# A mixture-of-experts tail with half-size tiles: tile plan, table in pieces, and results scattered by halves

## Chip, cores and metric

The kernel runs on one core of a Trainium2 chip. The metric is device time in microseconds (us) from the first to the last instruction, as the median of three runs. All arithmetic is float32, so every product on TensorE appears in the trace as two matmul records with two weight loads.

## The reference

The input is an image batch `x` of shape (2, 256, 56, 56). Layer 0 is a group norm, a convolution that makes queries, keys and values, a windowed attention and a projection. Layer 1 turns the image into 6272 tokens of 256 features, runs a linear attention with a feed-forward block, and then a mixture of experts. The change is about that last part:

```python
logits = xt @ Wr + br                         # 6272 tokens, 8 experts
top_p, top_idx = jax.lax.top_k(softmax(logits), 2)
weights = top_p / top_p.sum(axis=-1, keepdims=True)
xe = xn[None] * ln_g[:, None, :] + ln_b[:, None, :]
h = gelu(einsum('end,edh->enh', xe, W1) + b1[:, None, :])   # 256 -> 1024
y = einsum('enh,ehd->end', h, W2) + b2[:, None, :]          # 1024 -> 256
out = (weights[:, :, None] * y_of_the_two_chosen).sum(axis=1)
t = t + out
```

Every token goes to 2 of the 8 experts, so there are 12544 (token, expert) rows. How many fall to each expert depends on the data.

## The kernel before

**Stages.** `front` does layer 0. `layer1` does the rest of the attention in groups of tokens, up to 4 blocks of 128 tokens each, in the order of the list `order`: eleven groups of four blocks, then groups of one, two and two blocks, 14 groups and 49 blocks in all. For each group there are generators: `queries` (q), `message` (m), `feed_forward` (f) and `route` (r); `route` has three steps, and the third of the group before is called p. A string of letters for each step `s` says in which order TensorE gets their parts: `turns` for the steps with new groups, `last` for the steps that drain the pipeline. TensorE's order is the written one (`manual_schedule`); the other engines' queues are ordered by a scheduler.

**Routing.** `route` normalises a group, computes the router (L1663), picks two experts (`top_two`, L1592), counts the rows of each expert in `cnt`, and scatters each token's normalised row twice into a table `xs` in HBM with indirect DMAs on GpSimd (POOL). Each expert has its own region in `xs`.

**Experts.** Class `Experts` works on tiles of `ST` = 256 rows of one expert. Which expert and which rows a tile takes is decided on the chip: `full_tiles` (L1195), called once after the first `NE` = 36 blocks have been counted, makes a table A of `NTA` = 29 tiles that are certainly full by then; `other_tiles` (L1209), called in the fifth tile of the main loop, makes a table B for all further ones from the final counts, and writes one block of filler rows behind each expert's rows (8 DMAs). Both use `table` (L1149), a chain of small VectorE (DVE) instructions. A tile goes through these steps:

- `fetch` (L1235): SyncE (SP) reads the tile's expert and row from the table into registers, then issues four DMAs in this order: the rows `xr` (260 KB), the weights `w1e` and `w2e` (1 MB each) and the bias `b2e`. The weights have two buffers, so `w1e` of a tile can only be loaded once the first product of the tile two before it is done, and `w2e` once its second product is done. DVE makes the weight of each row (`eq`) and its token number (`idi`, two buffers).
- `turn` (L1274): 4 transposes on TensorE (`px`), then two DVE instructions that apply the expert's norm (`xe`).
- First product: 8 output pieces of 2 matmuls 128x128 by 128x256 (L1303), each followed by a Gelu on ScalarE (ACT, L1307).
- Second product: for each half of 128 rows 8 matmuls 128x128 by 128x256 (L1316).
- Result: one DVE add of the bias over both halves (L1323), then for each half a multiply by the row's weight on POOL (L1330) and an indirect DMA that adds the half onto `y2` in HBM (L158).

`NTL` = 56 tiles are enough for any counts. Three of them (0 to 2) are mixed with the end of the attention by the letter `e` in `last`; tiles 3 to 52 form the main loop; tiles 53 to 55 stand under a condition (`tc.If`, L1828) that is taken if the counts ask for them.

**Output.** From tile `NTE` = 43 on, `between` (L1810) reads a finished group of `y2` back (`read`, L1782) after the first product of each tile, and `write` (L1792) transposes the group read one tile before, copies it out of PSUM on ACT and stores it to `out` from the ACT queue. After the last tile the five remaining groups are read and written one after the other; the read buffers `yr` and the copies `o_sb` have two and three buffers.

Of the kernel before, what the change touches and what calls it, by code (L numbers as in the profile page):

```python
# [18 lines left out]
P = 128  # L19
# [28 lines left out]
NIF = 3  # L48
# [3 lines left out]
NE = 36  # L52
NTA = -(-(NE * P * K - E * (ST - 1)) // ST)
NTE = (NE * P * K + E * (ST - 1)) // ST
NTB = NTL - NTA
NFI = 3
# [3 lines left out]
def shape_constants():  # L60
# [24 lines left out]
    def key_masks(n, nk):  # L85
# [20 lines left out]
        "c_tile": np.tile(np.arange(NTA, dtype=np.float32), (P, 1)),  # L106
# [10 lines left out]
def hybrid_kernel(ctx: ExitStack, tc: tile.TileContext, a: dict, out: bass.AP):  # L117
# [981 lines left out]
    class Experts:  # L1099

        def __init__(self, ctx, tk):
# [12 lines left out]
            self.tnum = self.load("tnum", a["c_tile"], [P, NTA])  # L1116
            self.enum = self.load("enum", a["c_e"], [P, E])

# [11 lines left out]
        def counts(self, pc, ones, name):  # L1130

            nc.tensor.matmul(pc, ones, self.tk.cnt, start=True, stop=True)
            ce = self.wp.tile([P, E], F32, name=name)
            nc.vector.tensor_copy(ce, pc)
            return ce

        def steps_below(self, wp, ce, k0, op, name):

            ns = N // ST + 1 - k0
            gt = wp.tile([P, E, N // ST + 1], F32, name="gt")[:, :, :ns]  # L1140
            nc.vector.tensor_tensor(
                gt, ce.unsqueeze(2).to_broadcast([P, E, ns]),
                self.steps[:, k0:].unsqueeze(1).to_broadcast([P, E, ns]), op,
            )
            n = self.wp.tile([P, E], F32, name=name)
            nc.vector.tensor_reduce(n, gt, AX.X, ALU.add)
            return n

        def table(self, wp, name, tiles, nt, start):  # L1149
# [6 lines left out]
            nc.vector.tensor_reduce(incl, cum, AX.X, ALU.add)  # L1156

# [7 lines left out]
            nc.vector.tensor_tensor(more, base[:, 1:], base[:, :ns], ALU.subtract)  # L1165
            ge = wp.tile([P, tiles, ns], F32, name=f"ge{name}")
# [8 lines left out]
            nc.vector.tensor_scalar(et, et, float(E - 1), None, ALU.min)  # L1175
            etm = wp.tile([P, tiles], F32, name=f"etm{name}")
# [3 lines left out]
            nc.vector.tensor_tensor(ge, ge, more.unsqueeze(1).to_broadcast([P, tiles, ns]), ALU.mult)  # L1180
            rt = wp.tile([P, tiles], F32, name=f"rt{name}")
# [5 lines left out]
            nc.vector.tensor_copy(tab[:, 1, :], rt)  # L1187
            oh = wp.tile([P, tiles, E], F32, name=f"oh{name}")
# [6 lines left out]
        def full_tiles(self, pc, ones):  # L1195

            ce = self.counts(pc, ones, "ce1")
            nt = self.steps_below(self.wp, ce, 1, ALU.is_ge, "full")
            self.some = self.steps_below(self.wp, ce, 0, ALU.is_gt, "some")
            self.tab_a = self.table(self.wp, "A", NTA, nt, self.ebase)  # L1200

# [7 lines left out]
        def other_tiles(self, wp, pc):  # L1209
            ones = wp.tile([P, P], F32, name="ones4")  # L1210
            nc.vector.memset(ones, 1.0)
            ce = self.counts(pc, ones, "ce2")
# [4 lines left out]
            nc.vector.tensor_copy(endi, endf)  # L1217
            for e in range(E):
                r = self.value(endi[0:1, e : e + 1], E * RG - ST)
                ins = nc.sync.dma_start(xs[bass.ds(r, ST), :], a["c_fill"][e])  # L1220
                apart(ins.ins, [f"fill{self.tk.run}"], [f"xs{self.tk.run}", f"xfull{self.tk.run}"])
            n = self.steps_below(wp, ce, 0, ALU.is_gt, "all")
            nt = wp.tile([P, 2, E], F32, name="nt")
            nc.vector.tensor_tensor(nt[:, 0, :], self.some, self.taken, ALU.subtract)
            nc.vector.tensor_tensor(nt[:, 1, :], n, self.some, ALU.subtract)
            start = wp.tile([P, 2, E], F32, name="start")
            for k, t in enumerate((self.taken, self.some)):
                nc.vector.scalar_tensor_tensor(start[:, k, :], t, float(ST), self.ebase, ALU.mult, ALU.add)
            self.tab_b = self.table(
                wp, "B", NTB, nt.rearrange("p k e -> p (k e)"), start.rearrange("p k e -> p (k e)")  # L1230
            )
            self.last = wp.tile([P, 1], mybir.dt.int32, name="last")
            nc.vector.tensor_copy(self.last, self.tab_b.incl[:, 2 * E - 1 :])

        def fetch(self, t, pools):  # L1235

            run = self.tk.run
            full = t < NTA
            tab, k = (self.tab_a, t) if full else (self.tab_b, t - NTA)
            x = SimpleNamespace(t=t)  # L1240
            xr = x.xr = pools.xr()
            e = self.value(tab.tab[0:1, 0, k : k + 1], E - 1)
            r = self.value(tab.tab[0:1, 1, k : k + 1], E * RG + (NDUM - 1) * ST)
            ins = nc.sync.dma_start(xr, xs[bass.ds(r, ST), :].rearrange("(p j) c -> p j c", j=2))
# [16 lines left out]
            nc.vector.tensor_scalar(x.eq, xr[:, :, C + 3], tab.etm[:, k : k + 1], None, ALU.is_equal)  # L1261
            x.idi = self.small.tile([P, 2], mybir.dt.int32, name="idi")
            nc.vector.tensor_copy(x.idi, xr[:, :, C])  # L1263
            nc.vector.tensor_tensor(x.eq, x.eq, xr[:, :, C + 2], ALU.mult)
            nc.vector.tensor_tensor(x.eq, x.eq, xr[:, :, C + 1], ALU.add)
# [8 lines left out]
        def turn(self, x, pools):  # L1274

            px = pools.px()
            for ct in range(2):
                for j in range(2):
                    nc.tensor.transpose(px[:, ct, j, :], x.xr[:, j, ct * P : (ct + 1) * P], ident)
            x.xe = pools.xe()  # L1280
            for ct in range(2):
                nc.vector.tensor_scalar(
                    x.xe[:, ct, :], px[:, ct, :, :].rearrange("p j t -> p (j t)"),
                    x.sv[:, ct : ct + 1], x.sv[:, 2 + ct : 3 + ct], ALU.mult, ALU.add,
                )

        def run(self, ts, pools, between=lambda t: None):
# [3 lines left out]
            nxt = self.fetch(ts[0], pools)  # L1291
# [3 lines left out]
            for t in ts:  # L1295
                x = nxt
                if t < ts[-1]:
                    nxt = self.fetch(t + 1, pools)
                hT = self.w.tile([P, NJ, ST], F32, name="hT")
                for j in range(NJ):  # L1300
                    p1 = pools.ph()
# [8 lines left out]
                between(t)  # L1310
                if t < ts[-1]:
                    self.turn(nxt, pools)
                py = pools.py()
                for h in range(2):
                    for j in range(NJ):
# [4 lines left out]
                        if j % 4 == 3 and (h, j) != (1, NJ - 1):  # L1320
                            yield
                yt = pools.yt()
                nc.vector.tensor_tensor(yt, py, x.b2.unsqueeze(1).to_broadcast([P, 2, C]), ALU.add)  # L1323
                mine, others = [f"y{run}.{t}"], [f"y{run}.{t}"]
                if t < NTA:
                    mine, others = mine + [f"yfull{run}"], others + [f"ylate{run}"]
                if t >= NTE:
                    mine, others = mine + [f"yend{run}"], others + [f"yread{run}"]
                for h in range(2):
                    nc.gpsimd.tensor_scalar(  # L1330
                        yt[:, h, :], yt[:, h, :], x.eq[:, h : h + 1], 1.0, ALU.mult, ALU.mult
                    )
                    scatter(y2, x.idi[:, h : h + 1], yt[:, h, :], mine, others, compute_op=ALU.add)
                yield


    def layer1(ctx, tk, behind=(None, None)):
# [16 lines left out]
        early = next(i for i in range(len(order)) if sum(n for _, n in order[:i]) == NE)  # L1354
        with lin as ph:
# [195 lines left out]
            def feed_forward(n0, n, m2T):  # L1551
# [13 lines left out]
                for k0 in range(0, n, 2):  # L1565
# [22 lines left out]
                    if (n0, n) in order[early:]:  # L1588
# [41 lines left out]
            def route(n0, n):  # L1630
# [57 lines left out]
                late = [f"xlate{run}"] if (n0, n) in order[early:] else []  # L1688
# [25 lines left out]
            last = "mefefpefmeferefer", "fefefpeferefeer", "eeeeprer", "eeeep"  # L1714
# [3 lines left out]
            with tc.manual_schedule(engines={mybir.EngineType.PE}):  # L1718
                on = {}
                for s in range(ng + 4):  # L1720
# [12 lines left out]
                    for part in turns[min(s, 2)] if s < ng else last[s - ng]:  # L1733
                        if part == "e":
                            next(tiles, None)
                        else:
                            next(on.get(part, iter(())), None)
                        if part == "p" and s == early + 3:
# [3 lines left out]
                            ex.full_tiles(ps_a.tile([P, E], F32, name="pc", tag="a"), ones)  # L1742
# [9 lines left out]
                            tiles = ex.run(range(NFI), pools)  # L1752
                            next(tiles)
# [10 lines left out]
        with ExitStack() as ph:  # L1764
            xp = ph.enter_context(tc.tile_pool(name="p4x", bufs=3, reuse_waits="tile"))
            yp = ph.enter_context(tc.tile_pool(name="p4yr", bufs=2, reuse_waits="tile"))
# [25 lines left out]
            def write(n0, n, yr, copy):  # L1792
                for ct in range(2):
# [5 lines left out]
                    o_sb = xp.tile([P, 512], F32, name="o_sb")  # L1799
                    copy(o_sb[:, : n * P], pt[:, : n * P])  # L1800
                    for b in range(B):
                        c0, c1 = max(n0 * P, b * T), min((n0 + n) * P, (b + 1) * T)
                        if c0 < c1:
                            nc.scalar.dma_start(
                                ov[b, ct, :, c0 - b * T : c1 - b * T], o_sb[:, c0 - n0 * P : c1 - n0 * P]
                            )

            held = []

            def between(t):  # L1810
                if t == NFI + 2:
                    ex.other_tiles(tp, ps_t.tile([P, E], F32, name="pc", tag="pt"))
                if t == NFI + 4 and run == 0:
                    check_sums(tp, ps_t)

                if t > NTE and held:
                    write(*held.pop(0), nc.scalar.copy)
                if NTE <= t < NTE + early:
                    held.append(read(*order[t - NTE], True))

            with tc.manual_schedule(engines={mybir.EngineType.PE}):
                for _ in ex.run(range(NFI, NTL - NIF), pools, between):
                    pass
            behind = nc.values_load(
# [64 lines left out]
```

## Time and profile before

| | |
|---|---|
| runs | 2144.49, 2147.65 and 2149.08 us |
| profiled execution | span 2144.9 us (2146.76 us by the clock of the runs) |
| TensorE (PE) busy | 1979.2 us, 92% of the span |
| DVE, ACT, POOL busy | 1007.1, 635.1, 692.1 us |
| expert tiles executed | 53 (1696 records each on L1303 and L1316) |
| first product, second product | 380.4 and 376.3 us busy |
| bytes moved by DMA | 265.93 MB, 124 GB/s over the span |

"Busy" is time with an instruction in progress. The slices of the page show busy tenths of an engine in 40 equal parts of 53.6 us; PEclk is the clock that TensorE was granted. In the timeline, a bracket at the end of a line says how long the engine stood idle before it and what released it. A row with PE gives the matmuls, PEld the weight loads, SPq and ACTq the issue of DMAs.

### The profile page before, as it was taken

The numbers are of one execution on the slowest core, as the hardware profiler recorded it, in microseconds if no ns is written. First come the engines' busy times: TensorE is split into PE (matmuls) and PEld (weight loads), VectorE is DVE, ScalarE is ACT, GpSimd is POOL, SyncE is SP. The second block draws the span as 40 slices with busy tenths as digits, with TensorE's granted clock in tenths as the row PEclk, the third lists the DMA queues.
The fourth block names the chain that finished last, engine by engine and source line by source line (L and its number), as shares of the span: only waits on it lengthen the run. The fifth ranks groups of instructions, "written<-read, shape, count | busy, mean of one in ns | idle before, by whom it ended". The sixth has DMA issues, their size and how long they took to land.

```text
span 2144.9 us, 27983 instructions
## 1 busy us (share of the span) xinstructions
PE 1979.2 (92%) x10190; PEld 1391.2 (65%) x10190; DVE 1007.1 (47%) x2538; ACT 635.1 (30%) x1256; POOL 692.1 (32%) x810
## 2 busy tenths in 40 slices
PE   6799989999988887999999979899999999999995
PEld 3454444554544555666656657688888888888884
DVE  6777877875986556455454454321111111111110
ACT  1233323233333222333233322322222222222231
POOL 4721012111013425345344444433323333233231
PEclk9999999999989999999999998999999999999997
DMA  5642422443243113001111131577666766677883
GB/s 130 156 105 74 144 73 65 116 124 87 88 133 80 49 29 109 11 21 40 35 50 48 50 131 48 173 221 212 196 186 199 200 192 188 195 204 207 251 242 98
DMA packets 189461, 265.93 MB, mean 124 GB/s; under 512 B 25335, under 2 KB 148549, under 8 KB 189071
## 3 DMA queue, kind: packets, MB, share of 16 engines
q1 hardware_dynamic: 161694, 221.74, 34.3%
q0 software_dynamic: 21296, 30.41, 7.2%
q10 hardware_dynamic: 6320, 11.86, 1.8%
q8 instruction: 84, 1.38, 0.3%
q14 instruction: 67, 0.54, 0.1%
HBM read 197.01 MB, written 71.21 MB: 125 GB/s over the span
## 4 chain that ended last, share of the span: by engine, by line
PE 30%; issue 25%; DVE 16%; POOL 15%; DMA 6%; ACT 3%; SPq 0%; POOLq 0%; DVEq 0%; ACTq 0%
POOL y L158 7%; PE p L1559 4%; PE py L501 4%; PE pc L513 4%; PE po L566 4%; DMA y<-yt,idi 3%; DVE yc L526 3%; DVE p L557 2%; POOL rs L246 2%; PE s_ps L553 2%; POOL yt L1330 2%; PE kp L277 2%; PE s_ps L350 1%; PE kx L290 1%; PE py L1571 1%
## 5 line engine op out<-in xcount | busy, mean ns | idle before, releaser
L1303 PE MATMUL ph<-xe,w1e 128*128 128x256 f32 x1696 | 380.4, 382 | 13.3 <-ACT hT L1307 9.0
L1316 PE MATMUL py<-w2e,hT 128*128 128x256 f32 x1696 | 376.3, 380 | 0.0
L1303 PEld LDWEIGHTS ph<-xe,w1e 128*128 128x128 f32 x1696 | 323.6, 191 | 58.9 <-ACT hT L1307 9.4
L1307 ACT ACTIVATE hT<-ph,sv 128x256 f32<-128x256 f32 x424 | 201.0, 474 | 540.2 <-PE ph L1303 537.1
L1316 PEld LDWEIGHTS py<-w2e,hT 128*128 128x128 f32 x1696 | 318.6, 190 | 41.3
L526 DVE SCALAR_TENSOR_TENSOR yc<-ypad,w,yc 128x1120 f32<-128x1120 f32 x192 | 267.1, 1394 | 46.8 <-ACT yc L524 43.8
L513 PE MATMUL pc<-ypad,diag 128*128 128x448 f32 x432 | 176.6, 549 | 0.5 <-ACT ypad L507 0.5
L158 POOL DMA_INDIRECT y<-yt,idi x106 | 168.6, 1591 | 25.3 <-issue 16.1
L501 PE MATMUL py<-x_sb,wq 128*128 128x448 f32 (+1 forms) x384 | 157.2, 541 | 14.9 <-ACT yc L517 9.5
L562 ACT ACTIVATE p<-p 98x680 f32<-98x680 f32 (+5 forms) x120 | 111.8, 932 | 179.5 <-DVE p L557 173.7
L557 DVE TENSOR_TENSOR p<-s_ps,tab 98x340 f32<-98x340 f32 (+5 forms) x240 | 137.9, 600 | 56.8 <-PE s_ps L553 55.4
L1263 DVE CAST idi<-xr 128x2 int32<-128x2 f32 x53 | 9.0, 169 | 317.9 <-DMA y<-yt,idi 317.9
L1330 POOL TENSOR_SCALAR yt<-yt,eq 128x256 f32<-128x256 f32 x106 | 49.3, 472 | 310.4 <-DVE yt L1323 305.2
L1323 DVE TENSOR_TENSOR yt<-py,b2e 128x512 f32<-128x512 f32 x53 | 36.6, 692 | 234.9 <-PE py L1316 234.9
L553 PE MATMUL s_ps<-qT,kT 32*98 32x170 f32 (+5 forms) x960 | 130.5, 402 | 16.9 <-DVE p L557 15.6
L553 PEld LDWEIGHTS s_ps<-qT,kT 32*98 32x98 f32 (+1 forms) x960 | 57.4, 170 | 104.3 <-DVE p L557 58.2
L513 PEld LDWEIGHTS pc<-ypad,diag 128*128 128x128 f32 x432 | 78.2, 189 | 71.7 <-issue 67.8
L490 POOL TENSOR_SCALAR diag<-ident,w 128x128 f32<-128x128 f32 x108 | 84.6, 801 | 116.4 <-PE pc L513 109.5
L501 PEld LDWEIGHTS py<-x_sb,wq 128*128 128x128 f32 x384 | 71.0, 198 | 78.7 <-issue 55.5
L158 POOL DMA_INDIRECT xs<-row,si x98 | 96.1, 981 | 64.2 <-DVE si L1687 33.0
L246 POOL TENSOR_TENSOR rs<-rs,mhalf 128x2 f32<-128x2 f32 (+2 forms) x89 | 65.2, 739 | 145.5 <-DVE rs L245 122.6
L1559 PE MATMUL p<-m2T,fw 128*128 128x512 f32 (+2 forms) x224 | 94.3, 544 | 0.0
(326 smaller groups left out, 2594.0 us busy)
## 6 DMA issues: line engine op xcount, KB each, us to landing
w1e<-in_L_ffn_W SPq DMA_DIRECT2D x53, 1024.0 KB
w2e<-in_L_ffn_W SPq DMA_DIRECT2D x53, 1024.0 KB
yd<-yc SPq DMA_DIRECT2D x24, 784.0 KB
xr<-xs SPq DMA_DIRECT2D x53, 260.0 KB
ld<-yd SPq DMA_DIRECT2D x28, 448.0 KB
b2e<-in_L_ffn_b SPq DMA_DIRECT2D x53, 128.0 KB
yr<-y SPq DMA_DIRECT2D x11, 512.0 KB
out<-o_sb ACTq DMA_DIRECT2D x22, 256.0 KB
```

The lines of the kernel that those rows point to most:

```text
L158: ins = nc.gpsimd.indirect_dma_start(out=dst[:, :], out_offset=bass.IndirectOffsetOnAxis(ap=index, axis=0), in_=src, in_offset=None, **kw,)
L246: nc.gpsimd.tensor_tensor(r[:, :n], r[:, :n], mhalf[:, :n], ALU.pow)
L501: nc.tensor.matmul(py[:, :n, :], wq1[:, ct, oc * P : (oc + 1) * P], x_sb[:, ct, (q0 + g0) * WW : (q0 + g0 + n) * WW], start=(ct == 0), sto ...
L513: nc.tensor.matmul(pc, diag[:, tap, :], ypad[:, dy : dy + 8, dx : dx + WW], start=(tap == 0), stop=(tap == 8),)
L526: nc.vector.scalar_tensor_tensor(yc[:, 8:, :], src, w, yc[:, 8:, :], ALU.mult, ALU.add)
L553: nc.tensor.matmul(s_ps[:nk, j, :n].rearrange("p (i j) -> p i j", j=nj), kT[hs], q[hs], start=True, stop=True,)
L557: nc.vector.tensor_tensor(p[:nk, 2 * pr : 2 * pr + 2, :n].rearrange("p h (i j) -> p h i j", j=nj), s_ps[:nk, :, :n].rearrange("p h (i j) - ...
L562: nc.scalar.activation(p[:nk, :, :n], p[:nk, :, :n], AF.Exp)
L1303: nc.tensor.matmul(p1, x.w1[:, ct, j * P : (j + 1) * P], x.xe[:, ct, :], start=(ct == 0), stop=(ct == 1),)
L1307: nc.scalar.activation(hT[:, j, :], p1, AF.Gelu, bias=x.sv[:, 4 + j : 5 + j])
L1316: nc.tensor.matmul(py[:, h, :], hT[:, j, h * P : (h + 1) * P], x.w2[:, j, :], start=(j == 0), stop=(j == NJ - 1),)
L1559: nc.tensor.matmul(p1[:, :w], fw1[:, k, oc * P : (oc + 1) * P], rhs, start=(k == 0), stop=(k == 3))
```

## The change

1. **Tile plan.** 48 full tiles and 5 half tiles (128 rows of one expert) take the place of the 53 full tiles. A half tile has half of the transposes, first products of 128x128 by 128x128, Gelus of 128 columns and one half of the second product; its DMAs of `w1e`, `w2e` and `b2e` are those of a full tile. An expert gets a half tile where its last tile is new after 36 blocks and has 128 rows or less; a third table H lists them. The half tiles stand between the last full ones: 43, h0, 44, h1, 45, h2, 46, h3, 47, h4. Everything beyond 48 full and 5 half tiles (8 full, 3 half) stands under the condition.
2. **First count a group sooner.** Table A is made after 32 blocks (`NE1`), with 25 tiles. The counts after 36 blocks (`NE2`) are kept by a copy (`remember`). The letter strings begin mixing `e` one step earlier.
3. **Tables in pieces.** `table`, `full_tiles` and `other_tiles` are generators, stepped once after each part of the order. `other_tiles` starts in the first tile of the main loop instead of the third, and its eight filler DMAs are issued one by one.
4. **Results by halves.** `turn` makes bias times weight on POOL ahead; after each half of the second product one DVE instruction makes `py * eq + yt`, and that half is scattered at once. `idi` has four buffers.
5. **Output.** `yr` has five buffers, `o_sb` a pool of its own with four. In the loop, the write of the group read before stands ahead of the next read. At the end all five reads are issued first; the two halves of a group are copied by ACT and DVE and stored from the ACT and the SP queue.

```diff
-NE = 36
-NTA = -(-(NE * P * K - E * (ST - 1)) // ST)
-NTE = (NE * P * K + E * (ST - 1)) // ST
+NE1, NE2 = 32, 36
+NTA = -(-(NE1 * P * K - E * (ST - 1)) // ST)
+NTE = (NE2 * P * K + E * (ST - 1)) // ST
+NFS, NHS = 48, 5
...
         def full_tiles(self, pc, ones):
-            ce = self.counts(pc, ones, "ce1")
+            ce = self.counts(self.wp, pc, ones, self.tk.cnt, "ce1")
             nt = self.steps_below(self.wp, ce, 1, ALU.is_ge, "full")
-            self.some = self.steps_below(self.wp, ce, 0, ALU.is_gt, "some")
-            self.tab_a = self.table(self.wp, "A", NTA, nt, self.ebase)
+            yield
+            self.tab_a = yield from self.table(self.wp, "A", NTA, nt, self.ebase)
+            yield
...
         def other_tiles(self, wp, pc):
+            nc.vector.tensor_scalar(fit, n, -float(ST), float(ST - P), ALU.mult, ALU.add)
+            nc.vector.tensor_tensor(fit, fit, ce, ALU.add)
+            nc.vector.tensor_scalar(half, fit, 0.0, None, ALU.is_le)
+            nc.vector.tensor_tensor(half, half, late, ALU.mult)
+            yield
...
+            self.tab_h = yield from self.table(wp, "H", E, half, start[:, 2, :])
...
             for e in range(E):
+                yield
                 r = self.value(endi[0:1, e : e + 1], E * RG - ST)
                 ins = nc.sync.dma_start(xs[bass.ds(r, ST), :], a["c_fill"][e])
...
         def turn(self, x, pools):
...
+            x.yt = pools.yt()
+            for h in range(nh):
+                nc.gpsimd.tensor_scalar(x.yt[:, h, :], x.b2, x.eq[:, h : h + 1], 1.0, ALU.mult, ALU.mult)
...
                 py = pools.py()
-                for h in range(2):
+                for h in range(nh):
                     for j in range(NJ):
                         nc.tensor.matmul(
...
-                        if j % 4 == 3 and (h, j) != (1, NJ - 1):
+                        if j == 3:
                             yield
-                yt = pools.yt()
-                nc.vector.tensor_tensor(yt, py, x.b2.unsqueeze(1).to_broadcast([P, 2, C]), ALU.add)
...
-                for h in range(2):
-                    nc.gpsimd.tensor_scalar(
-                        yt[:, h, :], yt[:, h, :], x.eq[:, h : h + 1], 1.0, ALU.mult, ALU.mult
+                    nc.vector.scalar_tensor_tensor(
+                        x.yt[:, h, :], py[:, h, :], x.eq[:, h : h + 1], x.yt[:, h, :], ALU.mult, ALU.add
                     )
-                    scatter(y2, x.idi[:, h : h + 1], yt[:, h, :], mine, others, compute_op=ALU.add)
-                yield
+                    scatter(y2, x.idi[:, h : h + 1], x.yt[:, h, :], mine, others, compute_op=ALU.add)
+                    yield
...
-            last = "mefefpefmeferefer", "fefefpeferefeer", "eeeeprer", "eeeep"
+            last = "mqefpefemqfreferf", "meffefpemferfer", "fefpfefrefeer", "eeeeperer", "eeeep"
...
+            slots = [(t, 2) for t in range(NFI, NFS)]
+            for k in range(NHS):
+                slots.insert(len(slots) - NHS + k + 1, (k, 1))
+            first = slots.index((NTE, 2))
             held = []
-            def between(t):
-                if t == NFI + 2:
-                    ex.other_tiles(tp, ps_t.tile([P, E], F32, name="pc", tag="pt"))
...
-                if t > NTE and held:
-                    write(*held.pop(0), nc.scalar.copy)
-                if NTE <= t < NTE + early:
-                    held.append(read(*order[t - NTE], True))
+            def between(i):
+                if held:
+                    write(*held.pop(0), (nc.scalar, nc.scalar))
+                if first <= i < first + early2:
+                    held.append(read(*order[i - first], True))
...
-            with tc.If(behind > NTB - NIF):
-                for _ in ex.run(range(NTL - NIF, NTL), pools):
+            with tc.If(more > 0):
+                for _ in ex.run([(t, 2) for t in range(NFS, NTL)] + [(k, 1) for k in range(NHS, E)], pools):
                     pass
-            for h in held:
-                write(*h, evac)
-            for n0, n in order[early:]:
-                write(*read(n0, n, False), evac)
+            last = [read(n0, n, False) for n0, n in order[early2:]]
+            for h in held + last:
+                write(*h, (nc.scalar, nc.sync))
```

## The prediction

> **What bounds the kernel now.** I read the slices of the page first, for where TensorE (PE) isn't full; then busy time by stretches; then the timeline of each stretch that the change touches.
>
> ```profile
> PE   6799989999988887999999979899999999999995
> PEclk9999999999989999999999998999999999999997
> DMA  5642422443243113001111131577666766677883
> ...
> 1250.00:1300.00 50.00, 38.95 (x177) 30.12 (x176) 25.76 (x132) 9.37 (x28) 24.52 (x29) 0.83 0.44 151
> 1350.00:1400.00 50.00, 39.53 (x189) 33.76 (x188) 18.54 (x104) 15.20 (x29) 20.65 (x24) 0.90 0.60 178
> 1600.00:1650.00 50.00, 50.00 (x239) 44.01 (x239) 9.33 (x29) 11.86 (x25) 14.49 (x18) 1.00 0.64 187
> 2000.00:2050.00 50.00, 49.28 (x245) 43.15 (x246) 8.88 (x28) 14.90 (x31) 13.88 (x16) 1.00 0.85 246
> 2110.00:2130.00 20.00, 8.10 (x37) 6.72 (x36) 1.38 (x2) 0.00 (x1) 4.09 (x4) 0.76 0.36 92
> ```
>
> The columns of the stretches are length, PE, PE weight loads, DVE, ACT, POOL, PE's clock, DMA share, GB/s. Three regions follow. From 1406 to 2116 us PE is full with expert tiles: nothing but PE work itself counts. At 1250 to 1400, the end of the attention, PE waits and runs at a lowered clock. After 2116 the output is drained. Up to the first count, at about 1214, the two programs have the same order on every engine, so only these regions can change.
>
> ```profile
> 1255.56 1.22 PE L1498 MATMUL pd<-qz,ksm 128*128 128x256 f32 x2 [5.24 <-DVE m2T L172]
> 1256.58 3.62 PE L1559 MATMUL p<-xT_b,fw 128*128 128x512 f32 x4
> 1259.99 1.97 PE L1559 MATMUL p<-m2T,fw 128*128 128x512 f32 x4
> 1278.25 0.61 PE L1559 MATMUL p<-xT_ab,fw 128*128 128x128 f32 x4
> 1278.70 0.61 PE L1559 MATMUL p<-m2T,fw 128*128 128x128 f32 x4
> 1305.38 3.78 PE L1303 MATMUL ph<-xe,w1e 128*128 128x256 f32 x8 [3.08 <-DVE xe L1282]
> 1378.45 3.78 PE L1303 MATMUL ph<-xe,w1e 128*128 128x256 f32 x8 [8.98 <-ACT hT L1307]
> 2100.88 7.07 PE L1303 MATMUL ph<-xe,w1e 128*128 128x256 f32 x32
> 2108.66 7.07 PE L1316 MATMUL py<-w2e,hT 128*128 128x256 f32 x32
> ...
> 1375.43 0.17 DVE L1263 CAST idi<-xr 128x2 int32<-128x2 f32 x1 [6.49 <-DMA y<-yt,idi]
> ...
> 2123.50 10.06 SPq L1785 DMA_DIRECT2D yr<-y  x5
> ```
>
> The reader is to see that the wait of 8.98 us ends with ACT, but ACT was held by a DVE queue in which `idi` waited 6.49 us for a scatter to land; and that four records of 128 columns follow each other in 0.45 us (1278.25 to 1278.70), where 256 columns need 7.07/32, or about 0.22 us each.
>
> **What the Trainium skill says.** "TensorE: Matmul & The Clock Gate", What's actually happening: after an idle window of some 3.4 us the PE clock is halved until it has been busy for about as long. The trace agrees: after the 5.24 us wait four records take 3.62 us, later ones 1.97. The same page, Step-by-step: weights of the next matmul load while one runs. The trace agrees down to 128 columns: the 0.11 us a record above includes its load. "DMA: Bandwidth & Descriptors", Issuing engines are not separate DMA queues: moving stores from ACT's to SP's queue saves only issue time. No row of before shows output stores on SP. The same page, Specifications, gives HBM about 358 GB/s per core; this trace sustains 246 at a share of 0.85.
>
> **The change, part by part** (against the profiled span, 2144.9; the median of the runs, 2147.65, is 2.75 above it, so a difference carries over).
>
> *Tile plan.* I counted the reference's routing for these inputs on a host: 1542, 1397, 555, 1453, 1510, 2906, 1392, 1789 rows. In steps of 256 that is 53 tiles, as executed before. After 36 blocks all eight last tiles are still unopened; five have 128 rows or less. So 48 full and 5 half tiles are exactly enough. A steady full tile takes 14.25 us (first product at 1405.66 and 1419.91 in the timeline). A half: first product 32 records x 0.11 = 3.5, second 16 x 0.22 = 3.5, two transposes 0.2, together 7.15. Gelu on 128 columns is an ACT activation of 0.37 or less (hTl of the 128-row group) against 0.44 for PE per piece, so PE sets the pace. Saved on the path: 5 x 7.1 = **35.5**.
>
> *Its transfers.* Each half still brings 2.3 MB of weights and bias. Where the output is written, a full tile takes 15.58 us (2085.30 to 2100.88) and moves 3.8 MB. A pair of full and half needs 15.6 + 8.4 = 24.0 us of PE and moves 4.2 weights + 0.3 bias + 0.4 rows + 1.05 read + 1.05 written + 0.4 scattered = 7.4 MB: 306 GB/s. Scaling 246 at 0.85 gives 289 at 1; single slices of this stretch show 330. SP's order also bunches the first five reads of `y2` (2.6 MB) behind one fetch. From below, 0 (buffers give about a tile of slack). From above, only the present 245 GB/s: 30.2 us a pair, 6.2 lost in each of 4.5 pairs, 28. I take **5 lost**.
>
> *First count sooner, in pieces.* In the changed program's DVE order the 29 instructions of table A still stand together ahead of the copy `m2T`, one group sooner. So the 5.24 us wait and its slow clock (2.3) move, and nothing is gained: 0, from -2 to +6. Tile 0 enters PE one group sooner. Its first product then stands behind `xe`, which DVE has only after the feed-forward of another group (1285.5): about 6.5 us of waiting at 1280, where before 2.14 and 3.08 were waited; the later 3.08 for `xe` and its slow clock of 1.9 go. With four `idi` buffers DVE doesn't wait for the scatter, and the 8.98 and 2.4 of slow clock behind it go. Small waits of 1 for the router's transposes and 2.5 for tile 3's `xe` come in. Sum: 3.1 + 1.9 + 9.0 + 2.4 = 16.4 less 1.3 + 3.5 + 1 slow clock: about **11**, from -3 to 22. The filler DMAs and 13 more table instructions lie beside a full PE: `xe` has 7 us of second product to be made in, SP a tile of lead. 0, at most 2 lost.
>
> *The new wait on POOL.* Bias times weight waits for `b2e`, last of a fetch; queued behind it are the powers of the last groups and the scatters. In the loop `b2e` is issued 0.6 us after the tile before starts and needed a tile later. 0; in the attention's end up to 3 lost, inside the range above.
>
> *Results by halves and output.* Inside the loop nothing waits for the scatter. At the end: DVE 0.69, POOL 0.93 and two scatters at 1.9 each become DVE 0.48 (the same kind of instruction at L1580) and one scatter, 3.2 saved. The five reads now start together; before, buffers and transposes spread them over 10.06 us. The last read should land some 9 us after the first is issued instead of 13.8: 5 saved. Together **8**, from 4 to 11.
>
> Sum: 35.5 + 11 + 8 - 5 = 49.5 saved; 2147.65 - 49.5 = **2098 us**.
>
> **The rivals.**
> - *Transfers set the last ten slots* (0.13). For it: 306 GB/s wanted, 246 seen at a share of 0.85. Against: 330 in single slices, and PE never waited for weights at 0.85. At 245 GB/s: 28 lost instead of 5, 2121 us.
> - *The attention's end gives nothing* (0.15). For it: the table isn't broken up in DVE's order, and tile 0 meets a late `xe`. Against: the wait on `idi` surely goes. With -3 instead of 11: 2112 us.
> - *The plan doesn't fit and the condition is taken* (0.04), slower. 8 full and 3 half tiles behind the loop, 8 x 14.25 + 3 x 7.15 = 135 us on PE, so 2233. It decides from one row too many: the expert with 253 of 256 rows in its last tile is three rows away, and one half of 117 rows eleven. Against: routing in float32 would have to differ from the reference's in near ties, in one direction.
> - *Forecast* (0.68): 2098 us.
>
> **How the numbers follow.** The unknown terms give 2098 -22/+24: clock and tail can add 14, transfers can take 23. A range of 2080 to 2120 leaves out the branch and about half of the transfer case. It is faster in all but the branch: a chance of 0.95, with 0.01 for within 0.2% (4.3 us, about what a measurement of this kernel can tell from no change) and 0.04 for slower.
>
> **What would show it.** 1536 full-width records in the first product and 160 of 128 columns, half tiles of 7 to 9 us; a PE that stays at 49 of 50 us beside half tiles (transfers held) or shows waits on weights there, with a DMA share at 0.95 (they didn't); no wait on ACT of 9 us at the attention's end, but one of 5 for `m2T` a group sooner and one of 6 for `xe`; an end of some 21 us after the last product instead of 29. I'm wrong if PE waits more than 3 us a pair, or if further tiles run behind the loop.

## The result, and the profile after

The changed kernel takes 2160.96 us (median of four runs, 2157.64 to 2166.56), the kernel before 2146.30 beside it (2144.49 to 2149.08): a ratio of 1.007, 95% interval 1.0045 to 1.0094. Instead of 49.5 us less, it takes some 15 us more.

I cut both profiled executions at three places that each has: the start of the router's products of the last four-block group that both handle alike (`pl`, 1197.51 before), the first product of tile 3, and the end of the last expert product. "Two tiles" is the experiment `two_banks` below. Each column is one profiled execution.

| us | before | after | two tiles |
|---|---|---|---|
| start to router's products | 1197.5 | 1201.5 | 1205.5 |
| to tile 3's first product (attention's end) | 193.8 | 189.6 | 188.9 |
| to the end of the last expert product (main loop) | 724.4 | 738.2 | 691.3 |
| to the end | 29.2 | 26.6 | 26.5 |
| span | 2144.9 | 2155.8 | 2112.3 |

The first stretch holds the same work in the same order, and differs from execution to execution (1197.5 to 1211.8 us over all kernels of this study); I put none of it down to the change. Of the other three, two became shorter, by less than forecast; the main loop became 13.8 us longer, although five of its tiles were halved. The costliest groups of the page after show where (columns: line, engine, operation, form, count, busy us, mean ns, idle before it and what ended most of it):

```profile
L1371 PE MATMUL py<-w2e,hT 128*128 128x256 f32 x1616 | 372.5, 384 | 36.0 <-DVE yt L1377 36.0
L1353 PE MATMUL ph<-xe,w1e 128*128 128x256 f32 (+1 forms) x1696 | 362.3, 371 | 4.4 <-DVE qz L231 3.7
...
L1377 DVE SCALAR_TENSOR_TENSOR yt<-py,eq,yt 128x256 f32<-128x256 f32 x101 | 48.7, 483 | 271.3 <-PE py L1371 270.1
...
L1335 POOL TENSOR_SCALAR yt<-b2e,eq 128x256 f32<-128x256 f32 x101 | 47.1, 474 | 205.7 <-DMA b2e<-in_L_ffn_b 205.6
```

Second products wait 36.0 us for DVE's weighting of a half. Before, they waited for nothing (page before):

```profile
L1316 PE MATMUL py<-w2e,hT 128*128 128x256 f32 x1696 | 376.3, 380 | 0.0
```

The counts, 1696 and 1616, are those of 48 full and 5 half tiles: the plan fits. Stretches after (length, PE, weight loads, DVE, ACT, POOL, PE's clock, DMA share, GB/s):

```profile
1250.00:1300.00 50.00, 41.87 (x167) 29.63 (x163) 23.44 (x108) 14.76 (x41) 25.87 (x30) 0.90 0.23 79
1350.00:1400.00 50.00, 46.22 (x226) 39.64 (x225) 20.70 (x118) 17.60 (x34) 22.82 (x26) 0.97 0.56 161
1600.00:1650.00 50.00, 48.06 (x229) 41.37 (x228) 9.93 (x31) 12.94 (x28) 14.78 (x18) 1.00 0.67 182
2000.00:2050.00 50.00, 46.33 (x256) 40.52 (x255) 8.86 (x31) 15.46 (x36) 14.18 (x14) 1.00 0.88 280
2130.00:2150.00 20.00, 6.96 (x26) 4.55 (x26) 2.52 (x5) 2.18 (x5) 1.56 (x1) 0.61 0.59 181
```

From 1600 to 1650 us, where PE was full (50.00) and there is neither a half tile nor an output, it now has 48.06, and 229 records instead of 239. One tile in the timeline of PE, then DVE's instruction inside its gap:

```profile
1602.52 3.62 PE L1371 MATMUL py<-w2e,hT 128*128 128x256 f32 x16
1606.79 3.72 PE L1371 MATMUL py<-w2e,hT 128*128 128x256 f32 x16 [0.65 <-DVE yt L1377]
1610.34 7.07 PE L1353 MATMUL ph<-xe,w1e 128*128 128x256 f32 x32
1617.25 0.60 PE L1326 MATMUL px<-ident,xr 128*128 128x128 f32 x4
```

```profile
1606.25 0.48 DVE L1377 SCALAR_TENSOR_TENSOR yt<-py,eq,yt 128x256 f32<-128x256 f32 x1 [1.81 <-PE py L1371]
```

The first half's products end at 1606.14. DVE starts 0.11 us later, reads for 0.48, and PE starts the second half at 1606.79. So PE doesn't overlap with the reading of its own first half. A tile takes 15.17 us (transposes at 1602.08 and 1617.25) instead of 14.25: 0.65 idle, and 0.27 because two groups of 3.62 and 3.72 take that much longer than one of 7.07. For 45 full tiles of the loop this is 41 us.

### The profile page after: what moved, and what is told of

Read it like the earlier page. It is cut to its first block, busy times and chain, and to the rows that moved or that the text cites. A ratio compares the mean times of both kernels' runs of the same rounds, so it can differ in the third digit from the quotient of the medians.

```text
span 2155.8 us, 27909 instructions
## 1 busy us (share of the span) xinstructions
PE 1959.2 (91%) x10102; PEld 1360.1 (63%) x10102; DVE 1025.0 (48%) x2615; ACT 633.1 (29%) x1258; POOL 682.8 (32%) x800
## 4 chain that ended last, share of the span: by engine, by line
PE 60%; DVE 17%; DMA 6%; POOL 5%; ACT 3%; issue 3%; SPq 1%; DVEq 0%; POOLq 0%; ACTq 0%
PE py L1371 15%; PE ph L1353 14%; PE p L1608 5%; PE pc L515 4%; PE py L503 4%; PE po L568 4%; DVE yc L528 3%; PE s_ps L555 2%; DVE p L559 2%; DMA y<-yt,idi 2%; POOL rs L248 2%; PE s_ps L352 2%; PE kp L279 1%; PE kx L292 1%; DMA xr<-xs 1%
## 5 line engine op out<-in xcount | busy, mean ns | idle before, releaser
L1353 PE MATMUL ph<-xe,w1e 128*128 128x256 f32 (+1 forms) x1696 | 362.3, 371 | 4.4 <-DVE qz L231 3.7
L1357 ACT ACTIVATE hT<-ph,sv 128x256 f32<-128x256 f32 (+1 forms) x424 | 196.2, 463 | 562.1 <-PE ph L1353 559.3
L1371 PEld LDWEIGHTS py<-w2e,hT 128*128 128x128 f32 x1616 | 300.2, 191 | 91.6 <-DVE yt L1377 54.6
L1353 PEld LDWEIGHTS ph<-xe,w1e 128*128 128x128 f32 x1696 | 311.3, 191 | 45.2 <-DVE qz L231 3.8
L160 POOL DMA_INDIRECT y<-yt,idi x101 | 160.4, 1588 | 283.1 <-DVE yt L1377 144.7
L1377 DVE SCALAR_TENSOR_TENSOR yt<-py,eq,yt 128x256 f32<-128x256 f32 x101 | 48.7, 483 | 271.3 <-PE py L1371 270.1
L1309 DVE CAST idi<-xr 128x2 int32<-128x2 f32 (+1 forms) x53 | 9.6, 182 | 291.1 <-DMA xr<-xs 289.8
L1335 POOL TENSOR_SCALAR yt<-b2e,eq 128x256 f32<-128x256 f32 x101 | 47.1, 474 | 205.7 <-DMA b2e<-in_L_ffn_b 205.6
```

Of the source, the lines that this page charges most:

```text
L160: ins = nc.gpsimd.indirect_dma_start(out=dst[:, :], out_offset=bass.IndirectOffsetOnAxis(ap=index, axis=0), in_=src, in_offset=None, **kw,)
L1353: nc.tensor.matmul(p1, x.w1[:, ct, j * P : (j + 1) * P], x.xe[:, ct, :], start=(ct == 0), stop=(ct == 1),)
L1357: nc.scalar.activation(hT[:, j, :], p1, AF.Gelu, bias=x.sv[:, 4 + j : 5 + j])
L1371: nc.tensor.matmul(py[:, h, :], hT[:, j, h * P : (h + 1) * P], x.w2[:, j, :], start=(j == 0), stop=(j == NJ - 1),)
```

## The experiments

The edits are against the changed kernel where nothing else is said. Every time was measured beside the kernel before on the same chip, and a ratio is to that. Between experiments I compare the ratios; 0.001 of a ratio is 2.1 us.

**Is it the second half's wait, or the work that came with the halves?** `two_banks` gives each half its own PSUM tile (in the loop; tiles 0 to 2 keep one tile):

```diff
-                py=lambda: ps_y.tile([P, 2, C], F32, name="py2"),
+                py=lambda nh: [ps_y.tile([P, 2, C], F32, name="py2")[:, 0, :] for h in range(nh)],
...
-                            py[:, h, :], hT[:, j, h * P : (h + 1) * P], x.w2[:, j, :],
+                            py[h], hT[:, j, h * P : (h + 1) * P], x.w2[:, j, :],
```

> The changed kernel, with the two halves of the second product in two PSUM tiles of one bank each (the loop only; the first three tiles stay). Theory A (PE waits at the second half because DVE still reads the first half out of the same bank, and pays 15.17 - 14.25 = 0.92 us in each of 45 full tiles, 41 us): tile period back to 14.25, no wait on yt in the loop, about 2120 us. Rival B (the loss comes from what was added on POOL and DVE, products of bias and weight, scatters behind each half, and the wait only shows it): period stays near 15.2, within 5 us of the changed kernel's 2161. Rival C (the half tiles' transfers took it): the same, 2156 to 2161.

Measured: 2111.30 us, ratio 0.9835 (0.9807 to 0.9863). PE's timeline:

```profile
1602.58 7.07 PE L1371 MATMUL py<-w2e,hT 128*128 128x256 f32 x32
1609.49 7.07 PE L1353 MATMUL ph<-xe,w1e 128*128 128x256 f32 x32
1616.40 0.60 PE L1326 MATMUL px<-ident,xr 128*128 128x128 f32 x4
```

The two halves are one row of 7.07 us again, the period is 14.26 (1602.14 to 1616.40), and POOL's products and the scatters behind each half are all still there. B and C fall. It gave 50 us (0.0235 of 2149; 46.9 in the loops of the two profiles), more than 41, since not each wait costs 0.92: the loop's first tile alone waited 4.02 us, at a lowered clock after it (its second half took 5.41 us instead of 3.72). There the changed kernel's DVE had the pieces of `other_tiles`, which in the kernel before start only in the loop's third tile, in its queue ahead of the weighting: it worked on them after the first half had ended (1403.0), and the weighting started at 1406.50 (timeline of PE):

```profile
1399.38 3.62 PE L1371 MATMUL py<-w2e,hT 128*128 128x256 f32 x16
1407.02 5.41 PE L1371 MATMUL py<-w2e,hT 128*128 128x256 f32 x16 [4.02 <-DVE yt L1377]
```

In `two_banks` they stand ahead of it too (the weighting starts at 1409.60), and PE doesn't wait. So the shared tile also made PE pay for part three. `two_banks` was repeated as `two_banks_again`:

> two_banks once more, beside the others on one chip: ratio to the kernel before 0.9835 within 0.003, by every theory; the difference to two_banks_act_stores and to late_count_act_stores is then of one chip.

2115.08 us, ratio 0.9823 (0.9795 to 0.9852). Both intervals hold both values.

**The bank, or the tile?** `one_tile_two_banks` keeps one tile per result, twice as wide, so that each half lies in a bank of its own. The instruction order is that of the changed kernel:

```diff
-            ps_y = ph.enter_context(tc.tile_pool(name="p4py", bufs=2, space=PSUM, reuse_waits="tile"))
+            ps_y = ph.enter_context(tc.tile_pool(name="p4py", bufs=1, space=PSUM, reuse_waits="tile"))
-                py=lambda: ps_y.tile([P, 2, C], F32, name="py2"),
+                py=lambda nh: (lambda p: [p[:, h, :C] for h in range(2)])(ps_y.tile([P, 2, 2 * C], F32, name="py2")),
```

> The changed kernel, with the result of a tile as one PSUM tile that spans two banks, a half in each; one such tile instead of two. Its instruction order is that of the changed kernel. Theory A1 (the bank decides): as with two tiles, about 2120 us, no wait on yt in the loop. Theory A2 (the tile as the program names it decides, whichever banks it lies in): the wait stays, 2161 us, period 15.17.

Measured: 2163.03 us, ratio 1.0068 (1.0039 to 1.0098). Nothing is gained (PE's timeline, then DVE's):

```profile
1610.99 3.62 PE L1371 MATMUL py<-w2e,hT 128*128 128x256 f32 x16
1615.25 3.72 PE L1371 MATMUL py<-w2e,hT 128*128 128x256 f32 x16 [0.65 <-DVE yt L1377]
```

```profile
1614.71 0.48 DVE L1377 SCALAR_TENSOR_TENSOR yt<-py,eq,yt 128x256 f32<-128x256 f32 x1 [1.99 <-PE py L1371]
```

A1 falls, A2 holds: PE waits for the tile as the program declares it, whichever banks it lies in. Whether two halves in one bank could do without the wait wasn't tried, and no run here shows it. The Trainium skill says no ("PSUM — Partial Sum Buffer", PSUM bank collisions raise a hardware error): two engines on one bank and the same partitions at a time are an error even at different columns, so the guard has to be by bank. By that page and these runs together one needs both, two banks and two tiles. The Trainium skill, "Perfetto Trace Analysis", Optimizing Tensor Performance, Matmuls, has the remedy in one sentence: independent groups should rotate through PSUM banks so that the emptying of one overlaps the next. `two_banks` agrees, with 14.26 against 15.17 us a tile; `one_tile_two_banks` adds that the bank alone isn't enough.

**Part four alone, undone and done.** `after_whole_result` has the old result scheme (one DVE addition over both halves, then POOL's products and two scatters) in the changed kernel:

```diff
-                    nc.vector.scalar_tensor_tensor(
-                        x.yt[:, h, :], py[:, h, :], x.eq[:, h : h + 1], x.yt[:, h, :], ALU.mult, ALU.add
-                    )
...
+                nc.vector.tensor_tensor(
+                    yt[:, :nh], py[:, :nh], x.b2.unsqueeze(1).to_broadcast([P, nh, C]), ALU.add
+                )
```

> The changed kernel with part four undone: one DVE addition over both halves, then POOL's products and two scatters, as before the change; half tiles, count and output reading stay. Theory A: period 14.25, so 41 us less than 2161, and some 2 us back for the second scatter at the end: about 2122. If the attention's end suffers from the scatters by halves as well, down to 2112. Rival C (half tiles' transfers): 2150 or more.

2123.74 us, ratio 0.9898 (0.9864 to 0.9931), as A says; a steady tile takes 14.25 us (1603.68 to 1617.93). It is slower than `two_banks` by 0.0063 to 0.0075, 13 to 16 us: in the changed kernel, results by halves gain something once they have two tiles. By the stages of the two profiles some 10 us of it can be placed: 1.9 in the attention's end, 5.2 in the loop and 2.7 at the end.

`before_halves` puts the results by halves alone (`idi` keeps its two buffers) into the kernel before, one PSUM tile for both halves; `before_two_banks` the same with two:

> The kernel before with part four alone: results weighted and scattered by halves, both in one bank. Theory A: 50 loop tiles x 0.92 = 46 us more than before's 2147, about 2190 us after some 2 us gained in the end. Rivals B and C: within 8 us of 2147 (C), or more than 2190 only if POOL sets the pace, with PE waiting on POOL or on scatters (B).

> The kernel before with part four alone, but the two halves in two tiles of one bank each in the loop. Theory A: no wait for yt in the loop, tile period 14.25; so not 2195 as with one tile, but before less 2.7 us at the end for one scatter instead of two, and up to 5 at the attention's end: 2142 to 2148 us. Rival B (POOL's products and scatters cost it): 2155 or more.

2194.61 us, ratio 1.0221 (1.0185 to 1.0258), with the same gap (timeline of PE in `before_halves`):

```profile
1601.34 3.62 PE L1324 MATMUL py<-w2e,hT 128*128 128x256 f32 x16
1605.60 3.72 PE L1324 MATMUL py<-w2e,hT 128*128 128x256 f32 x16 [0.65 <-DVE yt L1330]
```

and 2148.32 us, ratio 1.0000 (0.9987 to 1.0012). Rival B, which allowed for 2190 too, falls with the second: PE's 50 waits in the loop of `before_halves` are for `yt` of DVE, and they go with two tiles, though POOL's products and the scatters stay. So 0.022, some 47 us, are the shared tile in this kernel too. Done with two tiles, the halves neither cost nor gain in its time, though its profile has an end of 25.5 us after the last product instead of 29.2.

**The tile plan.** `two_banks_full_tiles` is `two_banks` with no halves:

```diff
-NFS, NHS = 48, 5
+NFS, NHS = 53, 0
...
-            nc.vector.tensor_scalar(half, fit, 0.0, None, ALU.is_le)
+            nc.vector.tensor_scalar(half, fit, -float(2 * ST), None, ALU.is_le)
```

> The kernel with the halves in two tiles of PSUM (two_banks, 2111 us), but with 53 full tiles instead of 48 full and 5 half ones. If the half tiles bring what step one says, 5 x 7.1 = 35.5 less the 0.9 us that PE waits for rows there: 2111 + 34.6 = 2146 us. Rival: transfers under the half tiles eat 5 us and more of it (step two): 2141 or less. Rival: the plan brings nothing: 2111.

2146.53 us, ratio 0.9986 (0.9972 to 1.0000). Against the two measurements of `two_banks`, the halves are worth 0.0151 and 0.0163 of 2149 us, 32 and 35 us. (The profile of `two_banks_full_tiles`, the slowest of its 12 runs, also lost 4.4 us once, in the loop's fourth tile, for rows that came late; why they did wasn't looked into.) The halves hold nearly the whole gain of `two_banks`: without them, all other parts together are at the edge of what can be told from none. The DMA does run full beside them (stretch of `two_banks`, then PE's longest wait there):

```profile
2000.00:2050.00 50.00, 48.18 (x272) 42.65 (x271) 10.71 (x38) 17.66 (x40) 14.38 (x17) 1.00 0.99 307
```

```profile
2005.02 3.93 PE L1353 MATMUL ph<-xe,w1e 128*128 128x128 f32 x32 [0.86 <-DVE xe L1329]
```

A share of 0.99 at 307 GB/s, and PE lost 0.9 us once, for an `xe` whose rows DVE had to wait for; weights never ended a wait of PE.

**The sooner count.** `two_banks_late_count` puts the first count back to 36 blocks, the table in one piece and the old letter strings:

```diff
-NE1, NE2 = 32, 36
+NE1, NE2 = 36, 36
...
-            last = "mqefpefemqfreferf", "meffefpemferfer", "fefpfefrefeer", "eeeeperer", "eeeep"
+            last = "mefefpefmeferefer", "fefefpeferefeer", "eeeeprer", "eeeep"
```

> two_banks with the first count where the kernel before has it (after 36 blocks, table in one piece, the strings of the attention's end as before); the four idi buffers and the halves stay. By step three 11 us slower than two_banks: 2122 us. By the traces (from the router's products of the same group to tile 3's first product 193.8 us before, 188.9 in two_banks): 5 slower, 2116. Rival: the gain is the idi buffers' alone and the sooner count only moves waits: 2108 to 2112.

2112.92 us, ratio 0.9828 (0.9802 to 0.9855): no difference to `two_banks` in the time. The attention's end can be read more finely from the profiles, one of each kernel, as the stretch of the table above:

| kernels | attention's end, us |
|---|---|
| count after 36, two `idi` buffers (before, `before_halves`, `before_two_banks`) | 193.8, 192.0, 193.3 |
| count after 32, four `idi` buffers (the nine other kernels) | 188.9 to 191.5, median 190.0 |
| count after 36, four `idi` buffers (`two_banks_late_count`, `late_count_act_stores`) | 186.5, 186.9 |

The sooner count costs some 3 us; the other edits give 6 to 7. That these come from the four `idi` buffers above all is argued from the next rows, not shown: the buffers weren't tried alone. PE's waits from 1200 to 1420 us, first before, then after (sum, times, longest):

```profile
PE ph L1303 <- ACT hT L1307: 9.0, 1, 9.0
PE pd L1498 <- DVE m2T L172: 5.7, 2, 5.2
PE ph L1303 <- DVE xe L1282: 3.9, 2, 3.1
```

```profile
PE pd L1547 <- DVE m2T L174: 8.4, 2, 4.2
PE pp L1727 <- DVE chosen L1719: 8.2, 1, 8.2
PE py L1371 <- DVE yt L1377: 5.7, 3, 4.0
PE ph L1353 <- DVE qz L231: 3.7, 1, 3.7
```

The 9.0 on ACT is gone (with two `idi` buffers and results by halves, in `before_halves`, it was still 3.7). In its place PE waits 8.2 us for `chosen`, which it did for 0.5 before, and twice 4.2 instead of once 5.2 for `m2T`.

**Why `chosen`?** The timeline of `two_banks` in that wait, DVE's row and then POOL's:

```profile
1341.53 0.88 DVE L1629 SCALAR_TENSOR_TENSOR u<-py,rs,g 128x256 f32<-128x256 f32 x2 [4.96 <-POOL rs L248]
```

```profile
1337.77 1.59 POOL L160 DMA_INDIRECT y<-yt,idi  x1 [0.30 <-issue]
1340.62 0.18 POOL L1703 COPY row<-dest 128x2 f32<-128x2 f32 x1 [1.26 <-DMA xs<-row,si]
1340.77 0.73 POOL L248 TENSOR_TENSOR rs<-rs,mhalf 128x2 f32<-128x2 f32 x1
```

The feed-forward's power `rs` stood on POOL behind eight row scatters, a result's scatter and a copy, and the router's instructions stood on DVE behind the reader of `rs`. `two_banks_pow_first` puts the eight scatters behind that power, in a step of their own:

```diff
-            nc.gpsimd.tensor_tensor(r[:, :n], r[:, :n], mhalf[:, :n], ALU.pow)
+            powers[:] = [nc.gpsimd.tensor_tensor(r[:, :n], r[:, :n], mhalf[:, :n], ALU.pow).ins]
...
+                with tc.issue_after(powers[0]) if (n0, n) == order[-4] else nullcontext():
```

> two_banks with the eight row scatters of the last four-block group put behind the power that the feed-forward needs, on POOL's queue, and the copy of the destinations one step later. Theory P (the 7.9 us that PE waits for 'chosen' come from that power standing in POOL's queue behind scatters): the wait falls to 1 to 4 us, and the kernel to 2104 to 2108 us. Rival D (it is DVE's own chain of small instructions, or the wait only moves to the next group): 2110 to 2113 us.

2114.69 us, ratio 0.9836 (0.9808 to 0.9864), and the wait rose from 7.9 to 9.9 us. The power now came in time (1337.27), but DVE then met the same scatters one link further on:

```profile
1343.15 0.75 DVE L239 BATCH_NORM_STATS2 st<-t_b 128x6 f32<-128x256 f32 x2 [3.57 <-POOL t_b L1635]
1347.58 0.16 DVE L1689 TENSOR_TENSOR u<-mv,rs 128x2 f32<-128x2 f32 x1 [3.20 <-POOL rs L250]
1350.81 0.59 DVE L1695 TENSOR_TENSOR sd<-u,rs 128x2 f32<-128x2 f32 x1 [2.00 <-POOL rs L1693]
```

So what theory P forecast, 1 to 4 us, failed, although the queue that it names is where DVE waits in both traces: DVE and POOL hand this chain back and forth four times, and about 10 us of scatters stand somewhere between. The wait only moved, as the second half of D said. An order with the sooner count and without this wait wasn't found; with the count after 36 blocks it is 1.0 us (`two_banks_late_count`).

**The end.** `two_banks_old_output` reads each late group only when the one before is written, with two `yr` buffers; `two_banks_act_stores` issues all stores of the drain from ACT, none from SP; `late_count_act_stores` has the late count as well:

```diff
-            yp = ph.enter_context(tc.tile_pool(name="p4yr", bufs=5, reuse_waits="tile"))
+            yp = ph.enter_context(tc.tile_pool(name="p4yr", bufs=2, reuse_waits="tile"))
```

```diff
-                            engines[ct].dma_start(
+                            nc.scalar.dma_start(
```

> two_banks with two buffers for the rows read back instead of five, and each late group read only when the one before it is written, as in the kernel before. By step five about 5 us slower (the reads together), 2116 us. By the traces (the end 26.6 us after the last product against 29.2, of which 2.2 lie in the single scatter): within 1 us, 2111 to 2112.

> two_banks with all stores of the drain issued by ACT (half of the copies still on DVE), none by SP. Theory S (the 2 us that the end lost again, 8.3 us from the last transpose's start to the end against 6.3 before, come from SP's stores, behind which SP still has to load the flag of the last branch): the stretch from the last expert product to the end falls from 26.6 to about 24.6 us, the time by 2 us. Rival: ACT's issue of ten stores in a row sets the end: 26 us or more.

> two_banks_act_stores with the first count where the kernel before has it. If the late count is worth the 2.4 us that the traces show (186.5 us against 188.9 from the router's products to tile 3's first product): 2 us below two_banks_act_stores, some 2107 us; if the sooner count is the better one, above it by up to 11 (step three).

| | time, us | ratio (95%) | end after the last product, us |
|---|---|---|---|
| `two_banks_old_output` | 2115.47 | 0.9844 (0.9823 to 0.9866) | 29.5 |
| `two_banks_act_stores` | 2108.63 | 0.9804 (0.9777 to 0.9830) | 25.5 |
| `late_count_act_stores` | 2107.21 | 0.9809 (0.9781 to 0.9837) | 25.4 |

The times don't tell these kernels apart from `two_banks`; one of the profiles' ends does. Seven profiles of kernels with all reads together and stores from SP end 25.8 to 26.6 us after the last product. Against them, reading together is worth some 3 us (29.5), between the 5 and the 1 that were expected. ACT's stores give 0.3 to 1.2 us, less than the 2 that S said and hardly more than the spread. Between the two readings of the late count (0.0005 apart) nothing can be told. Each of the last two is some 2% below the kernel before and, by ratios (0.9804 against 1.007), 2.6% below the changed one.

## Why the prediction was wrong, step by step

**The step that failed** is "Results by halves and output", and in it the sentence "Inside the loop nothing waits for the scatter", from which I took 0 for the loop. The sentence holds (PE waits for no scatter in the loop); I asked it of the wrong wait. The weighting by DVE stood between the two halves of one PSUM tile, and PE had to wait until it was read. I priced the queue behind the new instruction (DVE, POOL, scatters) and didn't ask who needs the buffer that it reads. The change itself carries the answer: `py` is taken once per tile, and the instruction that reads it now stands between the two groups of products that write it. So the stretch that I had called full of PE's work got a wait of its own. Measured: 0.92 us a steady tile, 47 to 53 us in all (by the loops of the profiles and by the ratios). With it alone mended, the kernel is at 2111 and 2115, inside the range and 13 to 17 above the forecast.

**The tile plan** was right: 48 and 5 fit, the condition isn't taken, 32 to 35 us where 35.5 was said. A pair takes 24.17 us in `two_banks` (2029.38 to 2077.71 for two), as forecast 24.0; in the changed kernel 25.20 (2020.38 to 2121.18 for four), since its full tile waits. My rule "wrong if PE waits more than 3 us a pair" didn't fire, as it looked for the fault only beside the half tiles.

**Its transfers** were sized too high: 5 said, 1 measured. The 289 GB/s that I scaled from a share of 0.85 were too low a ceiling, as the 330 in single slices hinted; the same stretch carried 307 in `two_banks`. The rival "transfers set the last ten slots" falls.

**The first count sooner** was mis-sized and partly of the wrong sign: 11 said; 4 in the profile. The 9 us on ACT went, as forecast, and tile 0's first product was late by less than feared (3.7, put down to `qz`, instead of 6.5 for `xe`). What I didn't have is the wait for `chosen` of 8.2 us and a second one for `m2T`. The measured 4 lies halfway between my 11 and the -3 of the rival "attention's end gives nothing"; for the sooner count taken alone, -3 is what the profiles show.

**The wait on POOL for `b2e`** cost nothing that the profile shows, as said: POOL stands 205.6 us for it, and in the loop of `two_banks` no product of PE waits behind it. Powers and scatters in one queue, which the same passage names, did cost at the attention's end, but by scatters in front of a power and not by `b2e`.

**The table's further instructions**, put at 0 to 2 beside a full PE, cost nothing with two tiles; with the shared tile they made the loop's first wait 4.02 us instead of 0.65.

**The end** was mis-sized: 8 said, 2.6 measured. From the last product to the issue of the reads 7.77 us became 5.75 (2.0 of the 3.2; the prediction's own terms give 3.0). From the reads to the first transpose 4.1 became 4.4. The transposes took 8.0 instead of 10.9 us (2.9 of the 5). And from the last transpose to the end 6.3 became 8.4. PE's rows of the end after:

```profile
2125.62 3.62 PE L1371 MATMUL py<-w2e,hT 128*128 128x256 f32 x16
2139.36 4.10 PE L1849 MATMUL pto<-ident,yr 128*128 128x128 f32 x17 [10.12 <-DMA yr<-y]
2144.09 2.17 PE L1849 MATMUL pto<-ident,yr 128*128 128x128 f32 x7 [0.63 <-DVE o_sb L1856]
```

For the 2 us lost at the very end the cause stays open. They were argued to be SP's, which stores now; but without its stores (`two_banks_act_stores`) at most 1.2 come back.

The sum: 2098, plus 50 for the second half's wait, 7 for the attention's end, 5 for the end, less 4 for transfers, is 2156; the runs have 2161.

## What to carry to other kernels

When an instruction that empties a result is moved into the middle of the products that fill it, ask first whether the products still to come write the same tile; then give each part its own PSUM tile in its own bank, or leave the emptying behind the last product. A gap of 0.65 us looks like nothing as one wait and decides the kernel when it comes once in each of 45 tiles. And when a wait at a busy crossing of two engines is taken away, look for the next link of the same chain before counting it as saved.

## What was not expected of the hardware and its program

- The wait follows the tile that the program declares: one tile over two banks waits as one bank does (15.17 us and 0.65 idle), two tiles in two banks don't (14.26 us).
- A stop of 0.65 us costs PE 0.92: 16 records take 3.62 and 3.72 us apart, 32 together 7.07.
- In `two_banks`, 307 GB/s at a DMA share of 0.99 pass beside a PE that is 96% busy (48.18 of 50 us), and PE waits for no weights.
- The first 1200 us, the same work in the same order, took 1197.5 to 1211.8 us from one profile to another. What varies there wasn't looked into. It is why differences below some 4 us were read from stretches and not from times; a stretch has one profile of each kernel, and nine of like order differ by 2.6 us at the attention's end.
